# Turning attention tokens by DMA and VectorE instead of TensorE in a two-layer gated cross-attention kernel

## The chip, the cores and the metric

The kernel runs on one core of one Trainium2 chip. The metric is the device time of one execution in microseconds; lower is better. A core has a matrix engine (TensorE, PE in the profile, with its weight loads as PEld), VectorE (DVE), ScalarE (ACT), GpSimd (POOL) and SyncE (SP), which here issues every DMA. Each engine works through its own instructions in order and waits on semaphores for the others.

## The reference

Everything is float32. `x` is 8 x 512 x 512 (4096 tokens of 512 features), the context is 8 x 120 x 512. Two layers of a gated cross-attention and a gated feed-forward part follow one another; attention has 16 heads of 32.

```python
x = x + tanh(g_xattn[0]) * L0_xattn(layernorm(x), ctx, ctx, ...)
x = x + tanh(g_ffn[0])   * L0_ffn(layernorm(x), ...)       # routed experts
x = x + tanh(g_xattn[1]) * L1_xattn(layernorm(x), ctx, ctx, mask, ...)
x = x + tanh(g_ffn[1])   * L1_ffn(layernorm(x), ...)       # channel mix

# attention
q = split_heads(Q @ W_q.T); k = split_heads(K @ W_k.T); v = split_heads(V @ W_v.T)
scores = einsum('bhqd,bhkd->bhqk', q, k) / sqrt(32)
out = einsum('bhqk,bhkd->bhqd', softmax(scores), v)
return merge_heads(out) @ W_o.T
```

The second attention also has biases and a key mask. The first feed-forward part picks, in each group of 32 tokens, one token for each of 128 experts; the second mixes each token with the one before it and multiplies by three matrices.

## The kernel before

`x` stays in SBUF as 32 tiles of 128 tokens (`NT = 32`, four tiles to a batch, `TB = 4`). One class, `CrossAttention`, serves both layers: it projects keys and values first (`project_keys`, `prologue`), runs three opening slots (`slot`), 24 steady slots (`steady(k)`, k from 4 to 27) and a tail. Instructions are issued in the written order on every engine (`manual_schedule`), so the order of calls in `steady` is the order on each engine and on SP's DMA queue.

Products of 512 x 512 are done as seven quarter products with sums of quarters (`SevenProducts`). `next()` runs one product on TensorE and takes it out of PSUM; `settle()` runs GpSimd additions that belong to product 7 and were put off. In a batch's four steady slots, seven products make the queries of the next batch: two in each of the first three, one in the fourth.

A steady slot k works on several tiles at once, in this order:

- `score_products(k)` on TensorE into two PSUM tiles, then `largest` on VectorE (negated maxima, L710);
- `turn_blocks(k-1, 0)`: VectorE turns 32 x 32 blocks of one half of the probabilities of tile k-1 (L793) and SP stores them to DRAM (`plane`, L796);
- `output(k-3)`: four 128-row chunks of the product with `wo` (L878), then VectorE adds the gated result to `x` (L888);
- `exponentials` on ScalarE (L721) and `divide` (a reciprocal on VectorE, L727, a multiplication on GpSimd, L731), half 1 and then half 0, with query products between them, and `turn_blocks(k, 1)`;
- `after(..., stage)` calls the next part of the network: in the first attention `RoutedFfn.in_slot`, in the second `ChannelMix.in_slot`. For the first, stage "final" stores `x` of tile k-3 to DRAM (`put_aside`, L1046), sums its statistics and computes its scales on GpSimd (`layernorm_scales`, L61 to L64: variance plus epsilon, power, product); stage "route" does router products of earlier tiles (L1074) and transposes a tile (L1065); stage "late" scales `x` on ScalarE (`route_scale`, L1052);
- `transpose_x(k+8)`: four TensorE transpositions of the normalized tile (L588) into PSUM, and a copy by ScalarE with the factor 1/sqrt(32) (L590) into `xnT`, which feeds the query products;
- `attend(k-2)`: probabilities times values (L861), copied by ScalarE to `aT`;
- `fetch_blocks(k-1)`: four loads bring the turned probabilities back from DRAM in the transposed layout (L806, `prT`, a single buffer);
- `normalize(k+9)` on ScalarE (L564), into one of two `xn` buffers.

PSUM tiles of products, outputs, transpositions and attend share four buffers in rotation (`p_mm`, tag "mm"); the scores have two of their own. The probabilities go through DRAM for tiles 4 to 25 (`CROSSED`); for the others TensorE turns them.

Of the kernel before, what the change touches and what calls it, by code (L numbers as in the profile page):

```python
# [31 lines left out]

KB, KF = 4, 30
CROSSED = range(TB, NT - TB - 2)


class Common:
# [15 lines left out]
    cm.nc.vector.bn_aggr(cm.mv[:, t, :], st)  # L53


def layernorm_scales(cm, pool, t, n):

    nc, ts = cm.nc, slice(t, t + n)
    mean, rstd, nmr = cm.mv[:, ts, 0], cm.rstd[:, ts, 0], cm.nmr[:, ts, 0]
    ve = pool.tile([P, TB], FP, name="ve")[:, :n]  # L60
    nc.gpsimd.tensor_scalar(ve, cm.mv[:, ts, 1], EPS, None, ALU.add)  # L61
    nc.gpsimd.tensor_tensor(rstd, ve, cm.mhalf.to_broadcast([P, n]), ALU.pow)
    if n == 1:
        nc.gpsimd.tensor_scalar(nmr, mean, rstd, -1.0, ALU.mult, ALU.mult)  # L64
    else:
        nc.gpsimd.tensor_tensor(nmr, mean, rstd, ALU.mult)
        nc.gpsimd.tensor_scalar(nmr, nmr, -1.0, None, ALU.mult)


def quarter(w, c, h, n=256):  # L70
# [150 lines left out]
class CrossAttention:  # L221
# [7 lines left out]
    def __init__(  # L229
        self, cm, tc, es, ins, gate, aside, mask=None, biases=None, loads=(), then=None,  # L230
        vpool=None,
    ):
        self.cm, self.nc, self.tc, self.gate, self.then = cm, cm.nc, tc, gate, then
        self.masked, self.biased = mask is not None, biases is not None

        self.aside, self.turned = aside, not loads
        nc = cm.nc

        def pool(name, bufs, **kw):
            if kw.get("space") != bass.MemoryType.DRAM:  # L240
# [16 lines left out]
        self.ops = {}  # L257
        self.biasless, self.opening = [], True

        def right(name):  # L260
            return tc.tile_pool(name=name, bufs=1, side="right", reuse_waits="tile")

        with right("at_v") as self.vp:
            with right("at_k") as self.kp:
                self.load(ins, list(loads), mask, biases)
                if self.biased:
                    self.scale_biases()
                self.project_keys()
                if self.masked:
                    self.make_mask()  # L270
            self.work = pool("at_work", 2)
            self.prologue()
        self.late = pool("at_late", 2)

    def load(self, ins, loads, mask, biases):
# [57 lines left out]
        for _ in range(2):  # L333
            if loads:
                loads.pop(0)()
        weights(self.wq, wqT)
        for more in loads:
            more()
        weights(self.wo, woT)
# [154 lines left out]
    def prologue(self):  # L494
# [27 lines left out]
            self.transpose_x(TB + t)  # L522
            self.normalize(TB + t + 2)
        for t in self.unmeasured:
            self.stats(t)
        q.next()
        rest = self.scores(0)

# [51 lines left out]
    def transpose_x(self, t):  # L580
# [2 lines left out]
        if i == 0:  # L583
            self.xnT[b] = self.work.tile([P, NC, S + 1], FP, name="xnT")
        xn = self.xn.pop(t)
        ps = self.p_mm.tile([P, NC, P], FP, name="xnps", tag="mm")
        for c in range(NC):
            nc.tensor.transpose(ps[:, c, :], xn[:, c * P : (c + 1) * P], self.cm.ident)  # L588
        dst = self.xnT[b][:, :, i * P : (i + 1) * P]
        nc.scalar.activation(dst, ps, AF.Copy, scale=SM_SCALE)  # L590
# [197 lines left out]

    def turn_blocks(self, t, u):

        nc = self.nc
        pr = self.probs[t][:, u * 1024 : (u + 1) * 1024]
        nc.vector.transpose(pr, pr)  # L793
        if u == 1:
            self.planes[t] = self.dram.tile([KB, P, 2, 256], FP, name="plane")
        nc.sync.dma_start(  # L796
            out=self.planes[t][:, :, u, :].rearrange("k p e -> p k e"),
            in_=pr.rearrange("p (k e) -> p k e", k=KB),
        )
# [1 line left out]
    def fetch_blocks(self, t):  # L801
# [1 line left out]
        prT = self.late.tile([P, 4, 512], FP, name="prT", bufs=1)  # L803
        plane = self.planes.pop(t).rearrange("k (q f) u e -> k f q (u e)", q=4)
        for k in range(KB):
            self.nc.sync.dma_start(out=prT[k:LK:KB], in_=plane[k, :KF])  # L806
        self.probs[t] = prT

    def transpose_probs(self, t):
# [118 lines left out]
    def steady(self, k):  # L928
# [45 lines left out]
        if done is not None:  # L974
            self.after(done, "late")

    def tail(self):

        for k in range(NT - TB, NT + 2):
            self.transpose_probs_late(k - 2)  # L980
            rest = self.scores(k) if k < NT else []
            self.output(k - 3, range(NC))
            self.after(k - 3, "final")
            self.after(k, "head")
            for part in rest:
                part()
# [3 lines left out]
            self.after(k, "end")  # L990
        self.output(NT - 1, range(NC))
        self.after(NT - 1, "final")
        self.after(NT - 1, "late")
        self.after(NT + 2, "end")


class RoutedFfn:
# [42 lines left out]

    def route_stats(self, t):
        layernorm_sums(self.cm, self.route, t)
        layernorm_scales(self.cm, self.route, t, 1)

    def put_aside(self, t):
# [333 lines left out]
class ChannelMix:  # L1379
# [56 lines left out]
    def in_slot(self, s, attention, stage):  # L1436
# [7 lines left out]
        if stage == "late" and s < NT - 2 * TB:  # L1444
            attention.scales(s)
        if s == -1:
            self.start()
# [379 lines left out]
```

## Time and profile before

| what | value |
|---|---|
| median of 3 runs | 1346.75 us (1345.57 to 1349.14) |
| profiled execution: time | 1344.31 us |
| profiled execution: span from first to last instruction | 1342.5 us |
| granted TensorE clock, mean | 0.999 |
| busy share of the span | TensorE 96%, VectorE 75%, ScalarE 60%, GpSimd 52% |
| bytes moved by DMA | 160.84 MB, mean 120 GB/s |
| TensorE transpositions of tokens, L588 | 256 instructions, 38.4 us busy |
| ScalarE copies of them, L590 | 64, 39.6 us busy, 619 ns each |

Stages can be told by the score products: attention 1's steady slots run from 113.59 to 369.51 us, attention 2's end with its tail's first transpositions at 978.34 us. The routed experts lie between the two, the channel mix after them. Durations in the trace are those of single instructions or of merged runs of them ("x4"). Because matmuls are pipelined, the spacing of one group's start to the next one's start tells more of TensorE than the length shown.

### The profile page before, as it was taken

The numbers are of one execution on the slowest core, as the hardware profiler recorded it, in microseconds if no ns is written. First come the engines' busy times: TensorE is split into PE (matmuls) and PEld (weight loads), VectorE is DVE, ScalarE is ACT, GpSimd is POOL, SyncE is SP. The second block draws the span as 40 slices with busy tenths as digits, with TensorE's granted clock in tenths as the row PEclk, the third lists the DMA queues.
The fourth block names the chain that finished last, engine by engine and source line by source line (L and its number), as shares of the span: only waits on it lengthen the run. The fifth ranks groups of instructions, "written<-read, shape, count | busy, mean of one in ns | idle before, by whom it ended". The sixth has DMA issues, their size and how long they took to land. (4 is left out here: it accounts for less than half of the span.)

```text
span 1342.5 us, 32823 instructions
## 1 busy us (share of the span) xinstructions
PE 1291.0 (96%) x13184; PEld 1024.3 (76%) x13184; DVE 1002.2 (75%) x1448; ACT 807.1 (60%) x2540; POOL 704.6 (52%) x626
## 2 busy tenths in 40 slices
PE   7999999999999988999999999999999999999997
PEld 6886777777766877888888667667666888888886
DVE  5876776777685776777887687777785778787776
ACT  1368888888774445455136778888774655544442
POOL 4856655565542002555797787777664333343332
PEclk9999999999999999999999999999999999999999
DMA  9501766766603256431410077767700000000000
GB/s 313 189 1 66 224 208 204 222 211 208 198 26 111 86 171 199 128 112 63 154 47 18 33 229 214 220 212 222 223 23 1 16 17 32 32 32 32 32 32 32
DMA packets 116237, 160.84 MB, mean 120 GB/s; under 512 B 6973, under 2 KB 71997, under 8 KB 116085
## 3 DMA queue, kind: packets, MB, share of 16 engines
q1 hardware_dynamic: 116085, 158.75, 37.1%
q8 instruction: 104, 1.70, 0.5%
q14 instruction: 48, 0.39, 0.1%
HBM read 93.84 MB, written 64.88 MB: 118 GB/s over the span
## 5 line engine op out<-in xcount | busy, mean ns | idle before, releaser
L721 ACT ACTIVATE pr<-s,nmx 128x120 f32<-128x120 f32 x768 | 273.5, 498 | 43.4 <-DVE nmx L710 25.1
L878 PE MATMUL ops<-wo,aT 128*128 128x512 f32 x512 | 237.0, 604 | 3.6 <-ACT aT L869 2.3
L731 POOL TENSOR_TENSOR pr<-pr,rs 128x960 f32<-128x960 f32 x88 | 160.1, 1820 | 139.9 <-DVE rs L727 138.0
L721 ACT ACTIVATION_READ_ACCUMULATOR pr<-s,nmx 128x1 f32 x768 | 195.3, 254 | 0.0
L878 PEld LDWEIGHTS ops<-wo,aT 128*128 128x128 f32 x512 | 91.9, 189 | 99.8 <-issue 89.2
L710 DVE TENSOR_REDUCE nmx<-s 128x8 f32<-128x960 f32 x96 | 106.6, 1153 | 57.9 <-PE s L666 57.8
L1353 POOL TENSOR_TENSOR r<-r,b 128x1024 f32<-128x1024 f32 x31 | 73.5, 2377 | 145.1 <-ACT r L1352 145.1
L793 DVE STREAM_TRANSPOSE pr<-pr 128x1024 f32<-128x1024 f32 x88 | 109.1, 1240 | 37.0 <-POOL pr L731 37.0
L165 PE MATMUL qps<-xnT,wq 128*128 128x256 f32 x512 | 119.0, 380 | 0.0
L165 PEld LDWEIGHTS qps<-xnT,wq 128*128 128x128 f32 x512 | 96.3, 189 | 23.3 <-issue 10.3
L52 DVE BATCH_NORM_STATS2 bnst<-x 128x6 f32<-128x512 f32 x128 | 87.5, 684 | 0.4
L1609 POOL TENSOR_TENSOR x<-x,cv 128x512 f32<-128x512 f32 x30 | 44.0, 1466 | 79.0 <-DVE cv L1606 79.0
L759 POOL TENSOR_TENSOR pr<-pr,rs 128x960 f32<-128x960 f32 x32 | 58.1, 1823 | 40.6 <-DVE rs L758 30.8
L861 PE MATMUL aps<-prT,v 120*32 120x128 f32 x2048 | 69.2, 276 | 7.6 <-DMA prT<-plane 3.9
L888 DVE SCALAR_TENSOR_TENSOR x<-ops,gates,x 128x512 f32<-128x512 f32 x64 | 47.8, 746 | 34.5 <-PE ops L878 34.1
L666 PE MATMUL s<-kT,qT 32*128 32x120 f32 x2048 | 71.8, 276 | 0.0
L666 PEld LDWEIGHTS s<-kT,qT 32*128 32x128 f32 x2048 | 65.7, 186 | 7.0 <-issue 4.9
L861 PEld LDWEIGHTS aps<-prT,v 120*32 120x32 f32 x2048 | 52.2, 109 | 21.2 <-issue 10.7
L1352 ACT COPY r<-rps 128x1024 f32<-128x1024 f32 x31 | 31.4, 1013 | 59.1 <-PE rps L1340 59.1
L1582 ACT ACTIVATE kT<-kT 128x512 f32<-128x512 f32 x32 | 20.0, 626 | 76.2 <-DVE kT L183 41.8
L1340 PE MATMUL rps<-ident,rT 128*128 128x128 f32 x512 | 61.9, 275 | 2.0 <-DVE rT L1320 1.7
L769 ACT ACTIVATE pr<-s,nmx 128x120 f32<-128x120 f32 x128 | 44.2, 371 | 29.0 <-DVE nmx L766 29.0
(239 smaller groups left out, 3134.4 us busy)
## 6 DMA issues: line engine op xcount, KB each, us to landing
plane<-pr SPq DMA_DIRECT2D x88, 512.0 KB, 3.5
prT<-plane SPq DMA_DIRECT2D x176, 240.0 KB, 4.1
w<-in_w_dram SPq DMA_DIRECT2D x32, 512.0 KB, 5.0
x<-in_x_dram SPq DMA_DIRECT2D x8, 1024.0 KB, 16.6
aside<-x SPq DMA_DIRECT2D x32, 256.0 KB, 3.1
x<-aside SPq DMA_DIRECT2D x8, 1024.0 KB, 9.7
out_dram<-x SPq DMA_DIRECT2D x14, 512.0 KB, 2.8
wk<-in_wk_dram SPq DMA_DIRECT2D x3, 1024.0 KB, 8.8
```

Source lines behind the costliest of these rows:

```text
L52: cm.nc.vector.bn_stats(st, cm.x[:, t, :])
L165: self.nc.tensor.matmul(ps[:, m, :], rows[:, k, m * n : (m + 1) * n], columns[:, k, :], start=(k == 0), stop=(k == 1),)
L666: nc.tensor.matmul(s[j // 2][:, j % 2, hc * LK : (hc + 1) * LK], self.qT[b][r : r + 32, hc, toks], self.kT[r : r + 32, hc, keys], start=no ...
L710: nc.vector.tensor_reduce(nmx[u], sv[u], AX.X, ALU.max, negate=True)
L721: nc.scalar.activation(dst, src, AF.Exp, bias=nmx[u][:, j, hc, :], accum_out=sm[:, u, j, hc : hc + 1],)
L731: nc.gpsimd.tensor_tensor(half[u], half[u], by, ALU.mult)
L759: nc.gpsimd.tensor_tensor(pr[:, js, :, :], pr[:, js, :, :], rs[:, js, :, :].to_broadcast([P, 2, NC, LK]), ALU.mult,)
L793: nc.vector.transpose(pr, pr)
L861: nc.tensor.matmul(out, self.v[b // 2][:LK, b % 2, h * HD : (h + 1) * HD], p, start=True, stop=True,)
L878: nc.tensor.matmul(ops, self.aT[t][:, c, :], self.wo[:, c, :], start=(c == 0), stop=(c == NC - 1),)
L1340: nc.tensor.transpose(ps[:, k // 4, (k % 4) * P : (k % 4 + 1) * P], self.rT[:, 16 * tq + 8 * h + k, :], self.cm.ident,)
L1353: nc.gpsimd.tensor_tensor(r, r, b2, ALU.add)
```

## The change

For tiles 14 to 31 of each attention (`MOVED`), the transposition on TensorE and its copy on ScalarE go. Instead `normalize` also stores the normalized tile to DRAM (`rows`), a slot later four DMAs load it back with 32-token blocks moved to partitions (`move_rows`, 64 KB each in runs of 512 bytes), and a slot after that VectorE turns its 32 x 32 blocks into `xnT`. The features of `xnT` then have another order, (q j e) with e and q on partitions, so `wq` is loaded in that order in four DMAs (`load_rows`), and the remaining tiles are normalized into that order. The factor 1/sqrt(32) moves from the copy into the scales (`measure`).

Beside this: `normalize` runs for tile k+10 in slot k; the scales of stage "final" become a stage of their own, "scales", after the second `divide`; the outputs of tiles 2 and 3 are split over two slots; the store of a tile's second half of probabilities (`store_blocks(k, 1)`) is issued after `fetch_blocks(k-1)`; and each fetch takes 32 rows of 128 partitions in all, where it took 30 of 120.

```diff
+MOVED = range(3 * TB + 2, NT)
...
-def layernorm_scales(cm, pool, t, n):
+def layernorm_scales(cm, pool, t, n, shrunk=1.0):
...
-    nc.gpsimd.tensor_scalar(ve, cm.mv[:, ts, 1], EPS, None, ALU.add)
+    nc.gpsimd.tensor_scalar(ve, cm.mv[:, ts, 1], EPS, shrunk, ALU.add, ALU.mult)
...
+def load_rows(nc, w, w_in):
+
+    rows = w_in.rearrange("(q j e) f -> q e j f", q=4, j=NC)
+    for q in range(4):
+        nc.sync.dma_start(out=w[32 * q : 32 * q + 32], in_=rows[q])
...
-        weights(self.wq, wqT)
+        load_rows(nc, self.wq, wqT)
...
-                self.stats(next(self.unmeasured))
+                self.measure(next(self.unmeasured))
...
+    def measure(self, t):
+        layernorm_sums(self.cm, self.norm, t)
+        if t % TB == TB - 1:
+            layernorm_scales(self.cm, self.norm, t - TB + 1, TB, SM_SCALE**-2)
...
         xn = self.norm.tile([P, D], FP, name="xn")
+        to, x = xn, cm.x[:, t, :]
+        if t not in MOVED:
+            to = xn.rearrange("p (j q e) -> p q j e", q=4, j=NC)
+            x = x.rearrange("p (q j e) -> p q j e", q=4, j=NC)
         nc.scalar.activation(
-            xn, cm.x[:, t, :], AF.Identity, bias=cm.nmr[:, t, :], scale=cm.rstd[:, t, :]
-        )
+            to, x, AF.Identity, bias=cm.nmr[:, t, :], scale=cm.rstd[:, t, :]
+        )
+        if t in MOVED:
+            self.rows[t] = self.dram.tile([P, D], FP, name="rows")
+            nc.sync.dma_start(out=self.rows[t], in_=xn)
...
         xn = self.xn.pop(t)
-        ps = self.p_mm.tile([P, NC, P], FP, name="xnps", tag="mm")
-        for c in range(NC):
-            nc.tensor.transpose(ps[:, c, :], xn[:, c * P : (c + 1) * P], self.cm.ident)
         dst = self.xnT[b][:, :, i * P : (i + 1) * P]
-        nc.scalar.activation(dst, ps, AF.Copy, scale=SM_SCALE)
+        if t in MOVED:
+            nc.vector.transpose(
+                dst.rearrange("p j (q t) -> p q j t", q=4),
+                xn.rearrange("p (q j e) -> p q j e", q=4, j=NC),
+            )
+        else:
+            ps = self.p_mm.tile([P, NC, P], FP, name="xnps", tag="mm")
+            for c in range(NC):
+                nc.tensor.transpose(ps[:, c, :], xn[:, c * P : (c + 1) * P], self.cm.ident)
+            nc.scalar.copy(dst, ps)
+        if t not in MOVED:
+            self.open_queries(t)
...
+    def move_rows(self, t):
+
+        xn = self.norm.tile([P, D], FP, name="xn")
+        quarters = self.rows.pop(t).rearrange("(i e) (q d) -> q e i d", e=32, q=4)
+        for q in range(4):
+            self.nc.sync.dma_start(
+                out=xn[32 * q : 32 * q + 32].rearrange("p (i d) -> p i d", i=4),
+                in_=quarters[q],
+            )
+        self.xn[t] = xn
...
-            self.nc.sync.dma_start(out=prT[k:LK:KB], in_=plane[k, :KF])
+            self.nc.sync.dma_start(out=prT[k::KB], in_=plane[k])
...
         if k - 1 in CROSSED:
             self.turn_blocks(k - 1, 0)
-        done = {TB: TB - 2, TB + 1: None}.get(k, k - 3)
-        if done is not None:
-            self.output(done, range(2 if done == TB - 1 else 0, NC))
+        if k + 8 in MOVED:
+            self.transpose_x(k + 8)
+        if k > TB + 1 and k + 9 in MOVED:
+            self.move_rows(k + 9)
+        done = k - 3
+        if k > TB:
+            self.output(done, range(0 if k > TB + 2 else 2, NC))
...
         divide(0)
+        if k > TB:
+            self.after(done, "scales")
...
         self.after(k, "route")
-        if k + 8 < NT:
+        if k + 8 in MOVED:
+            self.open_queries(k + 8)
+        elif k + 8 < NT:
             self.transpose_x(k + 8)
+            if k == TB + 1:
+                self.move_rows(k + 9)
         if k == TB:
             self.attend(k - 1)
-        elif k == TB + 1:
-            self.output(TB - 1, range(2))
-        else:
+        elif k > TB + 1:
             self.attend(k - 2)
+        if k < TB + 2:
+            self.output(k - 2, range(2))
         if k - 1 in CROSSED:
             self.fetch_blocks(k - 1)
-        if k + 9 < NT:
+        if crossed:
+            self.store_blocks(k, 1)
+        if k == TB:
             self.normalize(k + 9)
-        if done is not None:
+        if k + 10 < NT:
+            self.normalize(k + 10)
+        if k > TB:
             self.after(done, "late")
...
         if stage == "final":
             self.put_aside(s)
-            self.route_stats(s)
+            layernorm_sums(self.cm, self.route, s)
+        if stage == "scales":
+            self.route_scales(s)
```

The tail calls the stage "scales" right after "final", and `ChannelMix.in_slot` computes the next layer's scales in stage "scales" where it did so in "late".

More of the change, by code (lines that the diff above doesn't have):

```diff
@@ L256, in __init__ @@
         self.wide, self.planes = [], {}
-        self.ops = {}
+        self.ops, self.rows = {}, {}
         self.biasless, self.opening = [], True
@@ L524, in prologue @@
         for t in self.unmeasured:
-            self.stats(t)
+            self.measure(t)
         q.next()
@@ L585, in transpose_x, with open_queries @@
         xn = self.xn.pop(t)
-        ps = self.p_mm.tile([P, NC, P], FP, name="xnps", tag="mm")
-        for c in range(NC):
-            nc.tensor.transpose(ps[:, c, :], xn[:, c * P : (c + 1) * P], self.cm.ident)
         dst = self.xnT[b][:, :, i * P : (i + 1) * P]
-        nc.scalar.activation(dst, ps, AF.Copy, scale=SM_SCALE)
+        if t in MOVED:
[10 more added lines that the diff above has]
+            self.open_queries(t)
+    def open_queries(self, t):
+        b, i = divmod(t, TB)
         if i == TB - 1:
@@ L789, in turn_blocks, with store_blocks @@
     def turn_blocks(self, t, u):
-        nc = self.nc
         pr = self.probs[t][:, u * 1024 : (u + 1) * 1024]
-        nc.vector.transpose(pr, pr)
+        self.nc.vector.transpose(pr, pr)
+        if u == 0:
+            self.store_blocks(t, u)
+    def store_blocks(self, t, u):
+        pr = self.probs[t][:, u * 1024 : (u + 1) * 1024]
         if u == 1:
             self.planes[t] = self.dram.tile([KB, P, 2, 256], FP, name="plane")
-        nc.sync.dma_start(
+        self.nc.sync.dma_start(
             out=self.planes[t][:, :, u, :].rearrange("k p e -> p k e"),
@@ L961, in steady @@
         self.after(k, "route")
-        if k + 8 < NT:
+        if k + 8 in MOVED:
+            self.open_queries(k + 8)
+        elif k + 8 < NT:
             self.transpose_x(k + 8)
+            if k == TB + 1:
+                self.move_rows(k + 9)
         if k == TB:
             self.attend(k - 1)
-        elif k == TB + 1:
-            self.output(TB - 1, range(2))
-        else:
+        elif k > TB + 1:
             self.attend(k - 2)
+        if k < TB + 2:
+            self.output(k - 2, range(2))
         if k - 1 in CROSSED:
             self.fetch_blocks(k - 1)
-        if k + 9 < NT:
+        if crossed:
+            self.store_blocks(k, 1)
+        if k == TB:
             self.normalize(k + 9)
-        if done is not None:
+        if k + 10 < NT:
+            self.normalize(k + 10)
+        if k > TB:
             self.after(done, "late")
@@ L983, in tail @@
             self.after(k - 3, "final")
+            self.after(k - 3, "scales")
             self.after(k, "head")
@@ L992, in tail @@
         self.after(NT - 1, "final")
+        self.after(NT - 1, "scales")
         self.after(NT - 1, "late")
@@ L1042, in route_stats, with route_scales @@
         layernorm_sums(self.cm, self.route, t)
+        self.route_scales(t)
+    def route_scales(self, t):
         layernorm_scales(self.cm, self.route, t, 1)
@@ L1443, in in_slot @@
             attention.stats(s, False)
-        if stage == "late" and s < NT - 2 * TB:
+        if stage == "scales" and s < NT - 2 * TB:
             attention.scales(s)
```

## The prediction

> **What bounds the kernel now.** I read the page's busy line first, then a table of windows by stage, then one slot of the steady loop instruction by instruction, then the lists of waits and the DMA issue rows.
>
> ```profile
> PE 1291.0 (96%) x13184; PEld 1024.3 (76%) x13184; DVE 1002.2 (75%) x1448; ACT 807.1 (60%) x2540; POOL 704.6 (52%) x626
> ```
>
> An average over stages, so the steady slots need their own table. The rows are attention 1's slots 8 to 23 and 24 to 27, then attention 2's slots 4 to 7 and 8 to 23 (window, length, busy of PE, PEld, DVE, ACT, POOL, clock, DMA share, GB/s).
>
> ```profile
> 153.50:328.55 175.05, 170.56 (x1652) 125.87 (x1649) 128.38 (x216) 145.25 (x605) 102.45 (x106) 1.00 0.65 211
> 328.55:369.51 40.96, 40.86 (x401) 29.73 (x397) 28.86 (x51) 31.47 (x143) 25.16 (x26) 1.00 0.64 200
> 751.91:789.35 37.44, 33.27 (x338) 23.63 (x338) 27.12 (x39) 29.47 (x141) 28.83 (x24) 1.00 0.45 138
> 789.35:939.60 150.25, 149.57 (x1509) 103.96 (x1506) 114.22 (x169) 123.14 (x571) 111.74 (x88) 1.00 0.71 218
> ```
>
> TensorE is 97 to 99.8% busy in the steady rows, at full clock; every other engine has slack. So TensorE's work sets the slot. Attention 1's slots 24 to 27 transpose no tokens: a control. Their first lasts 10.52 us (scores at 328.55 and 339.07) against 10.96 for the same slot with a transposition (197.59 to 208.55).
>
> The end of one slot (scores at 231.80 and 241.03), from the timeline (start, length, engine, line):
>
> ```profile
> 239.05 0.60 PE L1065 MATMUL rxps<-ident,x 128*128 128x128 f32 x4
> 239.48 0.22 POOL L61 TENSOR_SCALAR ve<-mv 128x1 f32<-128x1 f32 x1
> 239.49 0.60 PE L588 MATMUL xnps<-ident,xn 128*128 128x128 f32 x4
> 240.02 1.08 PE L861 MATMUL aps<-prT,v 120*32 120x128 f32 x32
> 240.23 0.60 ACT L590 ACTIVATE xnT<-xnps 128x512 f32<-128x512 f32 x1
> 240.46 0.27 POOL L64 TENSOR_SCALAR nmr<-mv,rstd 128x1 f32<-128x1 f32 x1
> 240.85 1.82 POOL L731 TENSOR_TENSOR pr<-pr,rs 128x960 f32<-128x960 f32 x1
> 242.37 0.80 ACT L1052 ACTIVATE x<-x,nmr,rstd 128x512 f32<-128x512 f32 x1
> 243.46 0.47 ACT L721 ACTIVATE pr<-s,nmx 128x120 f32<-128x120 f32 x1 [0.29 <-DVE nmx L710]
> ```
>
> TensorE runs without a gap. GpSimd's three small scale operations (239.48 to 240.73) lie in the hole between its two divisions, and ScalarE's scaling L1052 finds them ready.
>
> The few real TensorE waits of the two attentions, then SP's issue rows (min/median/max ns) and VectorE's block transposition:
>
> ```profile
> PE aps L861 <- DVE qT L212: 3.3, 4, 0.8
> PE aps L861 <- DMA prT<-plane: 3.9, 4, 1.7
> L806 SPq DMA_DIRECT2D prT<-plane x176: 822/838/1888, 132.9 to 972.3; - x176
> L796 SPq DMA_DIRECT2D plane<-pr x88: 359/365/564, 123.4 to 964.6; - x88
> L1046 SPq DMA_DIRECT2D aside<-x x32: 320/337/1108, 101.6 to 427.7; - x32
> L793 DVE STREAM_TRANSPOSE pr<-pr 128x1024 f32<-128x1024 f32 x88 | 109.1, 1240 | 37.0 <-POOL pr L731 37.0
> ```
>
> **The change part by part.**
>
> *TensorE transpositions.* 18 tiles in each of two attentions lose four transpositions. Their price is the control's difference, 10.96 - 10.52 = 0.44 us a tile (slot 27 against slot 23: 8.80 against 9.23). 36 x 0.435 = 15.7 us off TensorE.
>
> [...]
>
> *ScalarE.* The copy L590 (0.60 us) goes for these 36 tiles. The normalization is as many operations as before; for other tiles it writes 32-element runs. L721 writes a strided layout too, at the same 0.34 us spacing as L769's dense one, so I take nothing.
>
> *VectorE.* One block transposition of 512 elements a tile: half of L793 is 0.62 us, a dense pass such as statistics on 512 is 0.68; bounds 0.62 to 1.24 (no gain from a longer queue), taken 0.65. It sits ahead of the output's addition L888, so that addition and the first reciprocal start some 0.45 us later. VectorE's busiest steady slot is 8.59 of 11.86 us, so the work fits; the cover is TensorE's 9 to 11 us.
>
> *PSUM.* The four-buffer rotation loses one user a slot. In the third slot of each four the attend product now takes the buffer released by L212, which waits on GpSimd (3.3 us above). Without the transposition tile it takes an earlier product's buffer. Those slots last 11.86 to 12.50 us; free of the stall they would be 10.53 (slot 26 shows 10.68).
>
> *Scales behind the second division.* This adds a wait. ScalarE's L1052 needs nmr, and behind it stand the next slot's exponentials. The new cycle in attention 1, from a slot's first exponential (each piece from rows at 821.22 to 829.51, where exponentials set the pace): eight exponentials to the reciprocal 2.93, to GpSimd's start 3.21, division to 5.03, turn L793 to 6.31, reciprocal and second division to 8.29, scales 1.33 (239.40 to 240.73) to 9.62, L1052 with hand-over 0.8: 10.42 us a slot. TensorE alone would need (8.80 + 10.53 + 10.96 + 10.53)/4 = 10.2. So this cycle, not TensorE, becomes attention 1's limit. In attention 2 no L1052 follows; its scales move earlier on GpSimd, worth nothing since ScalarE already has slack.
>
> *Attention 1 summed.* Slots 4 to 27 took 369.51 - 113.59 = 255.9 us, 10.66 a slot. 24 x 10.42 = 250.1, 5.8 less; the split output removes part of slots 4 to 7's idle time (39.91 long, 37.36 busy), 2 more. I take 7.5. Bounds: nothing gained if the cycle is 10.66; 12.7 if it never binds (18 x 0.435, and the third slots' stalls: 12.50 + 11.86 + 12.50 + 11.86 - 4 x 10.96 = 4.9).
>
> *Attention 2 summed.* Slots 8 to 23: three of four last 9.73 and become 9.30. The fourth (8.05 to 8.43) cannot follow: scores to first exponential 2.7, sixteen exponentials 5.35, then the scores' PSUM is free: 8.05. A cycle goes from 150.25/4 = 37.56 to 27.9 + 8.05 + 0.1 for a later VectorE = 36.05; times four, 6.0. Slots 4 to 7 idle 4.2 us: 1.38 for exponentials in the slot without output, which now gets half of one, 1.66 for a fetch that stood behind a store now queued after it. I take 3.0. Together 9.0; bounds 3 to 12.5.
>
> *SP's queue.* Each steady slot gains a store of rows, which waits for the normalization, and four loads, which wait for that store to land and for VectorE to release the tile; behind them stand put_aside and the four probability fetches, and TensorE's attend waits for these. The loop on SP is four fetches, two probability stores, a rows store, its landing, four loads, in attention 1 a put_aside. For the eight 32-partition issues the near rows are 0.34 (128 partitions) and 0.84 (30 partitions at a step of four): 2.7 to 6.7 us. With 0.72 for the stores, 0.34, and a landing of 3.1 (aside's median): 6.9 to 10.9. I take 0.36 apiece, since the loads have unit step and the fetch loses its odd 30: 7.0, below the 9.0 us slot; the cover is TensorE. The data, four times 0.26 MB of fetch, 1.05 MB stored, 0.52 MB new, is 2.6 MB a slot; at the 350 GB/s of 238 to 240 us it is 7.5 us, so that fits, with little to spare.
>
> [...]
>
> *The rest.* wq's load in four pieces of 256 KB, the same bytes, is needed some 30 us after it is issued; the zero rows add 64 KB to a fetch. I charge 0.5 us, bounds 0 to 2.
>
> Sum: 7.5 + 9.0 - 0.5 = 16 us. The profiled execution took 1344.31 us (span 1342.5, 1.8 around it), so it would take 1328.3; the median of the runs is 1346.75, 2.4 above it. I forecast 1346.75 - 16 = 1331.
>
> **The rivals.**
> - *TensorE stays the bound everywhere*, the scales' cycle overlaps better than I think: 12.7 + 12 = 24.7 us, 1322. For it: GpSimd is 59% busy there. Against: every piece of the cycle is in order on its engine.
> - *The scales' cycle eats attention 1's gain* (10.66 or more) and attention 2 gets only its 6: 1341. For it: ScalarE then idles in front of L1052.
> - *SP becomes the bound, slower.* If an issue of 32 partitions costs 0.84, the loop is 10.9 us in attention 2 against 9.4 now: 18 x 1.5 = 27 lost; attention 1's 11.2 against 10.66 loses 18 x 0.55 = 10: 1384. It decides from 8x + 4.16 = 9.4, x = 0.65 us. For it: prT's row; against: all rows with 128 partitions and unit step.
> - *The turn by VectorE does not shorten anything* because its tile arrives late: loads issued some 5.5 us into a slot must land by 4.7 us into the next, 8 us later; landings in the trace are at most 5.4. A slot without gain is 1346.
>
> **How the numbers follow.** Forecast (1326 to 1337) 0.46; TensorE bound throughout 0.18; cycle eats it 0.13; no gain 0.06; SP bound or another new stall 0.17. A change of 0.3%, 4 us, is about what a measurement of this kernel can tell from none. So faster 0.76, same 0.07, slower 0.17. The range takes 1318 (both upper bounds, 25, and 4 for stalls not listed) to 1347.
>
> **What would show it.** Right: L588 down from 256 to 112 instructions, spacing of scores in attention 2 at 9.30 three times of four; in attention 1 ScalarE waiting in front of L1052 for nmr, and a mean spacing near 10.4. Transposition near 0.65 us; the 32-partition issues near 0.36. Wrong: TensorE waiting for prT, VectorE waiting for xn from a DMA, SP's issues back to back, or spacing above 9.73 in attention 2.

## The result, and the profile after

The change made the kernel slower: 1393.66 us (median of 4 runs, 1391.38 to 1395.27) beside 1347.45 us for the kernel before in the same comparison, ratio 1.0343 [1.0329, 1.0357]. The forecast was 1331 us and faster. The profiled execution took 1391.38 us, with a span of 1389.4 us and a mean granted clock of 0.978 (0.999 before).

The busy line of the page, after:

```profile
PE 1301.3 (94%) x13040; PEld 1023.9 (74%) x13040; DVE 1018.5 (73%) x1484; ACT 788.1 (57%) x2504; POOL 702.3 (51%) x626
```

TensorE has 144 instructions fewer, as it should, and yet more busy time. The table of windows says where; attention 1's slots 8 to 23, then attention 2's, after (columns as in the prediction's table):

```profile
156.20:346.98 190.78, 173.28 (x1589) 125.01 (x1585) 135.78 (x229) 135.68 (x594) 101.54 (x105) 0.96 0.75 244
807.86:985.95 178.09, 156.30 (x1444) 104.86 (x1442) 124.05 (x186) 116.66 (x556) 111.52 (x89) 0.91 0.74 234
```

Against 175.05 and 150.25 us these stretches lost 15.7 and 27.8 us. In the second, TensorE idles 21.8 us where it idled 0.7. Its busy time should have fallen by 16 x 0.435 = 7.0 us and rose by 6.7, so an estimate puts 13.7 us of it down to the lower clock (0.91), by the price of 0.435. In the first, 13.0 us are added idle time and, by the same estimate, 9.7 the clock (0.96). Slots 4 to 7 lost 2.65 and 2.77 us, slots 24 to 27 1.1 and 0.4; the part between the two attentions gained 3.8. Together this is the 46.9 us of the span.

What TensorE waits for, from the list of waits of PE and then of SP's queue (us in total, times, longest), after:

```profile
PE aps L909 <- DMA prT<-plane: 24.4, 14, 3.1
```

```profile
SPq L633 <- DMA rows<-xn: 119.6, 33, 4.7
SPq L854 <- DMA plane<-pr: 28.6, 11, 6.0
```

TensorE waits for the fetched probabilities (3.9 us before). They come late because SP, in front of the loads L633, waits 33 times in 36 for the rows that it has just stored. One round of SP's queue in attention 1, from the timeline, after (start, length, line):

```profile
231.21 1.74 SPq L633 DMA_DIRECT2D xn<-rows  x4
233.05 0.38 SPq L1113 DMA_DIRECT2D aside<-x  x1
233.54 2.53 SPq L854 DMA_DIRECT2D prT<-plane  x4
236.17 1.36 SPq L844 DMA_DIRECT2D plane<-pr  x1
237.63 0.45 SPq L586 DMA_DIRECT2D rows<-xn  x1
238.17 1.20 SPq L844 DMA_DIRECT2D plane<-pr  x1
242.21 1.75 SPq L633 DMA_DIRECT2D xn<-rows  x4
```

It is busy back to back from 231.21 to 239.37 us. Then comes the hole, from 239.37 to 242.21: the store of 237.63 must land before the loads may go. The time from the start of a DMA's issue until its data have arrived is called its landing, 4.5 us here. The round closes on itself (loads, fetch, store, rows, landing, loads) and lasts 11.0 us here, with no TensorE in it. ScalarE had the tile ready long before the store's turn came; its normalization ended at 234.04, 3.6 us ahead of 237.63:

```profile
233.23 0.81 ACT L581 ACTIVATE xn<-x,nmr,rstd 128x512 f32<-128x512 f32 x1
```

Issue rows of the four (min/median/max ns), after, and the landing row of the rows' store (last number: median us):

```profile
L633 SPq DMA_DIRECT2D xn<-rows x144: 303/426/1666, 132.9 to 977.6; - x144
L854 SPq DMA_DIRECT2D prT<-plane x176: 577/603/1627, 135.6 to 1019.5; - x176
L844 SPq DMA_DIRECT2D plane<-pr x88: 359/539/1722, 123.4 to 1011.6; - x88
L586 SPq DMA_DIRECT2D rows<-xn x36: 320/448/942, 126.0 to 971.4; - x36
```

```profile
rows<-xn SPq DMA_DIRECT2D x36, 256.0 KB, 5.3
```

The loop by these rows: 4 x 0.43 + 4 x 0.60 + 2 x 0.54 + 0.45 + 5.3 = 10.95 us in attention 2, 11.3 with the put_aside in attention 1. The mean slots were 178.09/16 = 11.13 and 190.78/16 = 11.92.

### The profile page after: what moved, and what is told of

Read it like the earlier page. It is cut to its first block, busy times and chain, and to the rows that moved or that the text cites. A ratio compares the mean times of both kernels' runs of the same rounds, so it can differ in the third digit from the quotient of the medians.

```text
span 1389.4 us, 32889 instructions
## 1 busy us (share of the span) xinstructions
PE 1301.3 (94%) x13040; PEld 1023.9 (74%) x13040; DVE 1018.5 (73%) x1484; ACT 788.1 (57%) x2504; POOL 702.3 (51%) x626
## 5 line engine op out<-in xcount | busy, mean ns | idle before, releaser
L764 ACT ACTIVATE pr<-s,nmx 128x120 f32<-128x120 f32 x768 | 273.4, 497 | 45.9 <-DVE nmx L753 33.4
L926 PE MATMUL ops<-wo,aT 128*128 128x512 f32 x512 | 248.5, 627 | 3.6 <-ACT rxT L1134 1.5
L926 PEld LDWEIGHTS ops<-wo,aT 128*128 128x128 f32 x512 | 96.1, 199 | 105.8 <-issue 95.2
L909 PE MATMUL aps<-prT,v 120*32 120x128 f32 x2048 | 74.6, 290 | 38.0 <-DMA prT<-plane 24.4
L909 PEld LDWEIGHTS aps<-prT,v 120*32 120x32 f32 x2048 | 56.5, 115 | 55.6 <-issue 27.4
L709 PEld LDWEIGHTS s<-kT,qT 32*128 32x128 f32 x2048 | 74.3, 205 | 9.7 <-issue 7.1
L709 PE MATMUL s<-kT,qT 32*128 32x120 f32 x2048 | 80.6, 296 | 0.3 <-ACT pr L764 0.3
L917 ACT COPY aT<-aps 128x512 f32<-128x512 f32 x64 | 38.6, 603 | 46.4 <-PE aps L909 46.3
```

The costliest lines, as they stand in the source:

```text
L709: nc.tensor.matmul(s[j // 2][:, j % 2, hc * LK : (hc + 1) * LK], self.qT[b][r : r + 32, hc, toks], self.kT[r : r + 32, hc, keys], start=no ...
L764: nc.scalar.activation(dst, src, AF.Exp, bias=nmx[u][:, j, hc, :], accum_out=sm[:, u, j, hc : hc + 1],)
L909: nc.tensor.matmul(out, self.v[b // 2][:LK, b % 2, h * HD : (h + 1) * HD], p, start=True, stop=True,)
L926: nc.tensor.matmul(ops, self.aT[t][:, c, :], self.wo[:, c, :], start=(c == 0), stop=(c == NC - 1),)
```

## The experiments

All edits are made on the changed kernel unless another is named. Where an expectation names a theory by a letter: A is the rows' landing on SP's queue, C the scales' cycle through GpSimd, B the amount of data on the DMA engines, D the store of the second half behind the fetch, F the split outputs. Slot sums are us from one slot's scores to a later slot's, each from the profiled execution; ratios are to the kernel before, measured in the same comparison. A profiled execution is one of several and lies up to 6.4 us above its kernel's median (e4, e7) or 4.7 below it (e6). Stages that an edit doesn't touch differ by up to 3.1 us between two profiles (attention 2's slots 8 to 23 in e7 and e8), so a smaller difference of one stage settles nothing by itself.

| kernel | median us | ratio | att. 1, 8-23 | att. 2, 4-7 | att. 2, 8-23 |
|---|---|---|---|---|---|
| before | 1347.45 | 1 | 175.05 | 37.44 | 150.25 |
| changed | 1393.66 | 1.0343 [1.0329, 1.0357] | 190.80 | 40.21 | 178.09 |
| e1_fixed_rows | 1359.88 | 1.0082 [1.0065, 1.0098] | 172.46 | 40.89 | 165.30 |
| e2_early_norm | 1351.32 | 1.0026 [1.0008, 1.0044] | 169.47 | 40.03 | 157.23 |
| e3_no_moved | 1360.40 | 1.0081 [1.0060, 1.0103] | 174.57 | 40.56 | 157.60 |
| e4_scales_back | 1393.09 | 1.0339 [1.0312, 1.0366] | 191.29 | 39.83 | 181.11 |
| e5_no_moved_store | 1353.48 | 1.0043 [1.0030, 1.0055] | 174.72 | 40.33 | 150.47 |
| e6_early_store | 1353.71 | 1.0027 [1.0013, 1.0041] | 168.29 | 45.03 | 152.55 |
| e7_early_store_out | 1349.72 | 1.0005 [0.9986, 1.0024] | 168.23 | 44.20 | 156.04 |
| e8_early_store_out_scales | 1347.31 | 0.9985 [0.9963, 1.0007] | 165.57 | 42.44 | 159.13 |
| e9_first_only | 1334.38 | 0.9909 [0.9892, 0.9926] | 163.96 | 37.51 | 150.66 |
| e10_rows_act | 1352.61 | 1.0047 [1.0030, 1.0064] | 170.89 | 39.37 | 159.50 |
| e11_all_back_rows_act | 1341.71 | 0.9953 [0.9933, 0.9972] | 165.49 | 42.38 | 150.26 |
| e12_first_fetch | 1343.78 | 0.9957 [0.9943, 0.9971] | 167.40 | 42.79 | 148.30 |

**e1_fixed_rows: the loads without the landing in front of them.** The same stores and loads, but every load reads the rows of tile 12, written once; the moved tiles thus hold tile 12's tokens, and no load depends on the store of the slot before.

```diff
+        self.once = pool("at_once", 1, space=bass.MemoryType.DRAM)
...
+        if t == 12:
+            self.fixed = self.once.tile([P, D], FP, name="fixed")
+            nc.sync.dma_start(out=self.fixed, in_=xn)
...
-        quarters = self.rows.pop(t).rearrange(...)
+        self.rows.pop(t)
+        quarters = self.fixed.rearrange(...)
```

> The change, but the four loads of each tile read one DRAM tile that was written once in the opening slots (tile 12's normalized rows), so that SP does not wait for the landing of the store of the slot before. Stores, bytes, run lengths and number of issues stay; the moved tiles' contents are wrong. Theory A (SP's in-order queue: the wait for the landing, 3.2 us in the median, stands at the head of put_aside and the fetches and makes a loop of 11 us): attention 2's mean slot falls from 11.1 to 9.0-9.4 us, attention 1's from 11.9 to 10.2-10.7, time 1325-1345 us. Rival B (22 MB more on the DMA engines are too much): waits for prT stay, time 1380-1395. Rival C (the scales behind the second division hold ScalarE): attention 1 stays near 11.9, attention 2 is not touched, time 1380-1395.

Measured: 1359.88 us, 33.8 less than the changed kernel. The edit takes only the wait away (one more store of 256 KB comes in), so the wait for the landing holds most of the loss. It is not all: the time stays above the 1325 to 1345 us expected and above the kernel before, and SP now waits 70.0 us in front of the fetch for the plane store.

**e2_early_norm: the rows stored earlier in the slot.** The tile is normalized and its rows stored ahead of stage "route".

```diff
         self.q7.settle()
+        if k > TB and k + 10 < NT:
+            self.normalize(k + 10)
         self.after(k, "route")
...
-        if k + 10 < NT:
+        if k == TB:
             self.normalize(k + 10)
```

> The change, but in slots 5 and later the normalization of tile k+10 and the store of its rows are issued before the stage route, ahead of the fetch of the probabilities and of the second half's store, instead of behind both. Nothing is left out. Theory A: the rows have landed long before the next slot's loads ask, SP waits under 0.5 us there, attention 2's mean slot 9.0-9.4, attention 1's 10.2-10.7, time 1325-1345 us; ScalarE gets 0.8 us of work ahead of the copies, at most 0.4 us in the fourth slot of four. Rival B: no difference, 1380-1395. Rival C: attention 1 stays near 11.9, time 1380-1395.

Measured: 1351.32 us, above the 1325 to 1345 expected, but 42 below the changed kernel by an edit of place alone. The store now lands after 2.9 us (median) instead of 5.3, behind other work, and SP no longer waits for it: the list of SP's waits has no row of L633 for the rows, where the changed kernel's has 119.6 us. The bytes moved are the same, so rival B does not hold these 42 us.

**e3_no_moved: all of the change but the moved tiles.**

```diff
-MOVED = range(3 * TB + 2, NT)
+MOVED = range(NT, NT)
...
-            if k == TB + 1:
-                self.move_rows(k + 9)
```

> The change without its main part: no tile is turned by DMA (all 32 by TensorE, as before); normalization two tiles ahead, the late scales, the split outputs, the new order on SP, the 32-row fetches and the permuted layout stay. Theory A and rival B: what is left costs little, attention 2's mean slot 9.3-9.5, time 1338-1350 us. Rival C: attention 1's mean slot 11 or more, time 1352-1365.

Measured: 1360.40 us, 0.8% slower than before without a moved tile, where 1338 to 1350 was expected. From the list of waits of SP's queue, of this kernel:

```profile
SPq L854 <- DMA plane<-pr: 154.9, 64, 6.3
```

In front of the fetches SP stands until a plane store has landed, 154.9 us in all. Attention 1's slots 8 to 23 lose nothing by it (174.57 us), attention 2's lose 7.4. So the parts around the moved tiles have a cost of their own.

**e4_scales_back: the scales again at "final", with all the rest.**

```diff
         if stage == "final":
             self.put_aside(s)
-            layernorm_sums(self.cm, self.route, s)
-        if stage == "scales":
-            self.route_scales(s)
+            self.route_stats(s)
```

> The change with the first network's scales back ahead of the second division (stage final), all else as in the change. Theory A: attention 1 is held by SP, not by the scales, at most 4 us less: 1388-1394 us. Rival C: attention 1 falls from 11.9 to 10.9 a slot, 16 us less: 1374-1380. Attention 2 is not touched by this edit under either.

Measured: 1393.09 us, no change. While SP sets the slot the scales' wait is hidden.

**e5_no_moved_store: e3 with the second half's store back ahead of the fetch.**

```diff
     def turn_blocks(self, t, u):
...
-        if u == 0:
-            self.store_blocks(t, u)
+        self.store_blocks(t, u)
...
-        if crossed:
-            self.store_blocks(k, 1)
```

> No tile turned by DMA, and the store of a tile's second half of probabilities again issued as soon as it is turned, ahead of the fetch, as before the change; the rest of the change stays. Theory D (the new place of that store lets the fetch wait for a store that was issued late and stands behind 1.5 MB in the queues: 155 us of SP waits for plane in e3): SP's waits for plane fall under 20 us, attention 2's slots 8 to 23 from 157.6 to 150-151 us, time 1349-1353 us. Rival E (the split outputs and the order of slots 4 to 7 are all of it): slots 8 to 23 stay at 157, time 1358-1361.

Measured: 1353.48 us, and attention 2's slots 8 to 23 fall from 157.60 to 150.47, to what they were before. SP's waits for the plane are nearly gone, of this kernel:

```profile
SPq L853 <- DMA plane<-pr: 1.9, 2, 1.4
```

Issued behind the fetch (e3), the second half lands too late for the next slot's fetch: SP waited 154.9 us there and waits 1.9 here. That is D. What stays of 0.4% lies outside these slots: slots 4 to 7 take 2.4 us more than before in attention 1 and 2.9 in attention 2 (there 2.5 of it are busy time, at a clock of 0.92 instead of 1.00).

**e6_early_store: e2 with the same store edit as e5.**

```diff
# on e2
-        if u == 0:
-            self.store_blocks(t, u)
+        self.store_blocks(t, u)
...
-        if crossed:
-            self.store_blocks(k, 1)
```

> e2 (rows normalized and stored ahead of the fetch) with that store back ahead of the fetch too. Theory D: attention 2's slots 8 to 23 from 157.2 to 144-149 us, time 1336-1345 us. Rival E: 157 stays, time 1349-1353. Rival B (bytes): fetches arrive late in any order, 155 or more, time over 1348.

Measured: 1353.71 us: a miss, and not below e2's 1351.32. Attention 2's slots 8 to 23 gained 4.7 us (152.55, where 144 to 149 was expected), but slot 6 there grew from 12.6 to 16.3 us, and slots 4 to 7 took 5.0 back.

**e7_early_store_out: e6 with the outputs of tiles 2 and 3 where they were before.**

```diff
# on e6
-        done = k - 3
-        if k > TB:
-            self.output(done, range(0 if k > TB + 2 else 2, NC))
+        done = {TB: TB - 2, TB + 1: None}.get(k, k - 3)
+        if done is not None:
+            self.output(done, range(2 if done == TB - 1 else 0, NC))
...
-        if k < TB + 2:
-            self.output(k - 2, range(2))
+        elif k == TB + 1:
+            self.output(TB - 1, range(2))
```

> e6 with the outputs of tiles 2 and 3 in the slots where they were before the change. Theory F (the split outputs leave TensorE idle in slots 4 to 7: 42.9 us in e2 against 39.9 before in attention 1, 40.0 against 37.4 in attention 2, and a lower clock there): slots 4 to 7 return to 38-40 and 35-38 us, time 3-6 us below e6. Rival: those slots are held by the first loads and fetches, time within 1.5 us of e6.

Measured: 1349.72 us, 4.0 below e6 as F had it, though the intervals of the two overlap; but slots 4 to 7, where F put the gain, hardly move (42.76 to 42.88 in attention 1, 45.03 to 44.20 in attention 2). With moved tiles the split outputs do not hold them long, and F falls there.

**e8_early_store_out_scales: e7 with the scales back at "final".**

```diff
# on e7
-            layernorm_sums(self.cm, self.route, s)
-        if stage == "scales":
-            self.route_scales(s)
+            self.route_stats(s)
```

> e7 with the first network's scales back ahead of the second division. Theory C (scales, scaling of x and exponentials make a cycle of 10.4 us in attention 1): ScalarE's waits for nmr vanish (37 us in e2), attention 1's slots 8 to 23 from about 168 to 163-165 us, time 4-6 us below e7. Rival (TensorE's stall behind product 4 comes back, 4 x 1.2 us): within 1.5 us of e7 or slower.

Measured: 1347.31 us, 2.4 less than e7, where intervals overlap; but attention 1 shows it in its slots, 168.23 to 165.57 in 8 to 23 and 42.88 to 40.56 in 4 to 7. ScalarE's wait for nmr falls from 40.2 to 3.8 us. So C is real. Together these slots give 5 us; the stretch of 8 to 23 alone, 2.7 us, is within the spread of profiles, but the pattern is plain: the second slot of four takes 11.7 to 12.1 us in e7, from slot 9 on, and 10.96 in e8 from slot 13 on. The time of the whole kernel fell by less than the 4 to 6 us expected.

**e9_first_only: e8 with moved tiles in attention 1 alone.**

```diff
# on e8
+        self.moved = MOVED if loads else range(NT, NT)
...
-        if t in MOVED:
+        if t in self.moved:
...
-        if k > TB and k + 10 < NT:
+        if self.moved and k > TB and k + 10 < NT:
             self.normalize(k + 10)
```

In attention 2 it normalizes tile k+9 in its old place.

> Tiles turned by DMA in the first attention alone, rows normalized and stored ahead of the fetch (as e2), the second half's store, the outputs and the scales in their places of before; the second attention transposes on TensorE, normalizes one tile ahead, and keeps the permuted layout and the 32-row fetch. If theory A, C and D hold together: attention 1 as in e8 (slots 4 to 27 about 249 us against 257.8 before), attention 2 as before (slots 8 to 23 150 us, slots 4 to 7 37-38), time 1336-1341 us against 1347 before. Rival B (bytes on the DMA engines hold even the first attention): attention 1 at 255 or more, time 1345 or more.

Measured: 1334.38 us (1333.88 to 1335.21), faster than both kernels by more than the interval, and a little better than expected. The window of attention 1's slots 8 to 23, of this kernel:

```profile
156.69:320.65 163.96, 163.47 (x1588) 118.95 (x1584) 134.72 (x229) 135.82 (x588) 101.62 (x105) 1.00 0.86 283
```

TensorE is 99.7% busy at full clock in 163.96 us. The rival "TensorE stays the bound everywhere" put this stretch at 175.05 less 16 x 0.435 less 4.9 for the third slots: 163.2.

**e10_rows_act: the changed kernel, with the rows' store issued on ScalarE's queue.**

```diff
-            nc.sync.dma_start(out=self.rows[t], in_=xn)
+            nc.scalar.dma_start(out=self.rows[t], in_=xn)
```

> The change with one edit: the store of the normalized rows is issued on ScalarE's DMA queue instead of SP's, so that it does not stand behind the fetches and the second half's store in SP's order; bytes and all other orders stay. Theory A: the landing falls from 5.3 us to 2.0-3.5, SP's waits for rows from 120 us to under 30, time 1350-1365 us (the store of the second half behind the fetch still costs what e3 showed). Rival B: landings stay over 5 us since the engines are full, time 1385-1395.

Measured: 1352.61 us, 41 less. The landing row and SP's waits, of this kernel:

```profile
rows<-xn ACTq DMA_DIRECT2D x36, 256.0 KB, 3.6
```

```profile
SPq L844 <- DMA rows<-xn: 28.0, 12, 5.2
SPq L633 <- DMA rows<-xn: 4.9, 5, 1.7
```

The store has the same bytes, and lands after 3.6 us instead of 5.3, a little above what was expected. It is also issued earlier, and by more than that. In the changed kernel SP comes to it 4.1 us after the normalization has ended (median of 36); here ScalarE issues it as soon as it is done:

```profile
233.89 0.81 ACT L581 ACTIVATE xn<-x,nmr,rstd 128x512 f32<-128x512 f32 x1
234.74 0.33 ACTq L586 DMA_DIRECT2D rows<-xn  x1
```

So the run tests the store's place in the order of issue and its queue together, and not the queue alone; e2, on SP's queue, got as much from the place. In front of the loads SP waits 4.9 us instead of 119.6; the trace puts 28.0 us in front of a plane store down to the same landing, which leaves 32.9 in all. One word undoes nearly all of the loss.

**e11_all_back_rows_act: e8 with the rows' store on ScalarE's queue.**

```diff
# on e8
-            nc.sync.dma_start(out=self.rows[t], in_=xn)
+            nc.scalar.dma_start(out=self.rows[t], in_=xn)
```

> e8 (both attentions turned by DMA, rows early, second half's store, outputs and scales in their places of before) with the rows' store on ScalarE's DMA queue. If attention 2's slots 8 to 23 (159 us in e8, 150 before) are held by the rows' store standing ahead of the fetch on SP: 144-150 us, time 1332-1340. If they are held by the amount of data between one attend and the next (rival B, for attention 2 alone): 155-160 us, time 1344-1352.

Measured: 1341.71 us, between the two expectations. Attention 2's slots 8 to 23 fall from 159.13 to 150.26: the rows' store on SP did hold them. But 150.26 is only what they took before, though TensorE is 142.74 us busy there (149.57 before). Its 7 us came off and turned into idle time. And slots 4 to 7 stay at 42.38.

**e12_first_fetch: e11 with the first moved tile's loads behind the first fetch.**

```diff
# on e11
-            if k == TB + 1:
-                self.move_rows(k + 9)
...
             self.fetch_blocks(k - 1)
+            if k == TB + 1:
+                self.move_rows(k + 9)
```

> The kernel before this one (all parts undone but the moved tiles, rows stored by ScalarE's queue) with one edit: in the fifth slot of the steady loop the four loads of the first moved tile are issued behind the fetch of the probabilities instead of ahead of it. In that kernel attention 2's slots 4 to 7 took 42.38 us against 37.44 before, all of it in slot 6 (16.4 against 10.4), where TensorE waited 4.51 us for the first fetch, issued at 768.41 behind loads that took 2.17 us. If the loads ahead of the first fetch are the cause: the fetch is issued some 2.2 us earlier and lands without the loads' data in front of it, slot 6 falls to 11 to 13 us, attention 2's slots 4 to 7 to 37.5 to 39.5, and the time from 1341.7 to 1337 to 1339. If the cause is the store in front of them (the second half's store of tile 5, which VectorE turns late), slot 6 stays above 15 us and the time at 1340 to 1343. Attention 2's slots 8 to 23 stay at 150 in either case, since nothing in them is changed.

Measured: 1343.78 us (1340.27 to 1346.60), the same as e11. (Slot 6 took 11.5 us in the kernel before; the expectation's 10.4 is e9's.) Slot 6 of attention 2 falls from 16.4 to 14.0, between the two expectations, and slot 7 rises from 9.2 to 12.1. The fetch starts at 766.48 us instead of 768.41, and still TensorE waits. From the timelines of TensorE and SP, of this kernel:

```profile
773.31 1.93 PE L908 MATMUL aps<-prT,v 120*32 120x128 f32 x32 [3.71 <-DMA prT<-plane]
```

```profile
753.48 12.83 SPq L843 DMA_DIRECT2D plane<-pr  x3
```

The delay is moved, not removed. The stores ahead of the fetch end at 766.31, and the third of them waits for VectorE's turn of tile 5, which waits for GpSimd. In e9 the same three end 19.4 us behind slot 4's scores, here 21.8. GpSimd's timeline shows where these 2.4 us come from; here, and then in e9:

```profile
757.76 4.96 POOL L597 TENSOR_TENSOR x<-x,gbo 128x512 f32<-128x512 f32 x4
764.68 1.25 DVE L835 STREAM_TRANSPOSE pr<-pr 128x1024 f32<-128x1024 f32 x1 [4.75 <-POOL pr L774]
```

```profile
755.29 2.52 POOL L598 TENSOR_TENSOR x<-x,gbo 128x512 f32<-128x512 f32 x2
```

In the second attention each call of `normalize` also puts up to two additions of the output's bias on GpSimd (`add_bias`), ahead of the division that the turn waits for. Slot 4 calls it for tiles k+9 and k+10, so four additions stand there; e9's attention 2 calls it for one tile, and two do. The later turn thus comes from the normalization two tiles ahead and not from the moved tiles: e3 and e5, without any, have the same four additions. No run moved them, so what they cost in time is not shown.

## Why the prediction was wrong

**The step that failed** is the sum of SP's loop, 8x + 4.16 = 7.0 us, set below the slot of 9.0 so that SP cost nothing; the loop took 11 us and became the slot. Within it the term most short is the landing. It was taken as 3.1 us, the median of all put_asides; those of the steady slots stand some 1.0 us behind half a plane and 2.8 us behind the last of four fetches, and landed after 2.0 to 4.4, 3.4 in the median. The rows' store stands closer, mostly 0.6 us behind half a plane and 1.3 us behind a fetch of 1.05 MB, and landed after 5.3. The other terms were short too:

| term of the loop | predicted us | measured us | share of the miss |
|---|---|---|---|
| landing of the rows | 3.1 | 5.3 | 2.2 |
| eight issues of 32 partitions | 2.9 | 4.1 | 1.2 |
| two plane stores and a rows store | 1.06 | 1.53 | 0.5 |
| loop | 7.0 | 10.95 | 3.9 |

The landing is counted from the start of the issue. So the rows' own issue, and the next slot's first-half store that SP issues while it waits, lie inside it, and this sum counts them twice, as the prediction's did. By the timeline, attention 2's fifteen rounds from 800.57 to 971.41 us took 11.4 us each: 5.5 landing, 2.2 loads, 2.6 fetch, 0.8 from the fetch to the next rows' store, 0.3 between.

The rival "SP becomes the bound, slower" was the right one, for another reason than its own. It was to decide from x = 0.65 us; the mean of the eight issues is 0.51. With a landing of 3.1 the measured round would be some 11.4 - 2.4 = 9.0 us, an estimate, as long as the slot; no run shortened the landing inside the loop. What the runs show is the wait: e1 and e2 take the landing out of SP's loop, e10 nearly all of it, and 34, 42 and 41 of the 46 us came back. The prediction's own bounds for the loop, 6.9 to 10.9, reached above the slot already, with the landing held at 3.1; it took the lower end and called the rest cover.

**The new queue order had the wrong sign.** The prediction priced the second half's store behind the fetch as a gain of 1.66 us in attention 2's slots 4 to 7. e3 against e5, one edit apart, shows its cost: 7.1 us in attention 2's slots 8 to 23. It asked what the fetch gains and not who waits for the store: the next slot's fetch.

**TensorE's 15.7 us** were right as work. TensorE's busy time fell by 6.8 us in e11's sixteen slots, beside 7.0 by the price of 0.435. They became time in attention 1 alone (e9). There the steady slots, up to the tail's first transpositions, took 8.5 us less than before (247.4 beside 255.9; 7.5 forecast), but with the scales in their old place; with the late scales e6 and e7 have 2.8 and 2.7 us less.

**VectorE's block transposition** was taken as 0.65 us and took 0.67:

```profile
L608 DVE STREAM_TRANSPOSE xnT<-xn x36: 662/669/714, 142.7 to 980.1; 128x512 f32<-128x512 f32 x36
```

**The scales' cycle** of 10.42 us a slot was right as a limit and near in the mean, hidden in the changed kernel (e4) and seen in e7: 168.23/16 = 10.51. It is not an even 10.42, though: the second slot of every four takes 11.7 to 12.1 us where e9 has 10.96, and the others soon last what they last in e9. Putting the scales back gives 10.35 (e8) and 10.25 (e9, the same code in attention 1). So a part of the change worked against the gain.

**PSUM's third slots** lost their stall as forecast: attention 1's slots 10, 14, 18 and 22 took 12.50 and 11.86 us by turns and take 10.7 and 10.5 in e7 and e9 (10.53 forecast).

**Attention 2's 9.0 us** failed. Its cycle was to be three slots of 9.30 and one of 8.05. In e12's slots 8 to 23, eight of sixteen last 9.3 and the fourth ones 8.0 to 9.0, so the prices hold; but four last 9.5 to 10.4, and 148.30 us, in the fastest of twelve executions, is 2.0 less than before instead of 6.0. The 3.0 us of slots 4 to 7 never came: 40.3 to 40.6 us without any moved tile (e3, e5), above 37.44. e9's attention 2, with the outputs whole and one tile normalized ahead, is back at 37.51, so these two parts lengthen the slots together; which does how much was not tested. (In the prediction's table this row is 89% busy, 33.27 of 37.44, and not 97.)

**The fetch of 32 rows** fell from 0.84 to 0.60 us an issue, not to the 0.36 of the stores. That the odd 30 rows made the difference was the author's estimate, which no run shows: none changes the number of rows by itself. In place of the 0.36 us taken for all eight issues of 32 partitions, the median was 0.60 for the fetches and 0.43 for the loads at unit step; the plane stores took 0.54 in this kernel.

**What stays open:** why attention 2 keeps so little in slots 8 to 23, where TensorE idles 7.5 us in e11 and 4.6 in e12. In e11 and e12 its DMA share is 0.85 to 0.86, and so it is in e9's attention 1, which has its gain in full; a bound by the amount of data alone is therefore not shown. The single buffer prT was not tried with two.

## What to carry to other kernels

Before a load is put behind a store on the same queue, write the queue's loop with the landing in it, and take that landing from a store with as much data as close in front of it, not from a median over all moments (3.1 us was taken, 5.3 measured); a cover of 2 us in 9 needs both ends of every term. A store whose landing is waited for should be issued as soon as its data are ready, on another engine's queue (e10, 41 us less) or earlier on the same one (e2, 42 us less), so that its landing lies under other work. When several edits come together, take them one by one: here the moved tiles of one layer (e9: -0.9%) were a gain, and the rows' store behind the fetch, the new order of the plane stores, the later scales and the other layer's moves took it back.

## What the runs showed of the hardware

In attention 2 of the changed kernel TensorE's granted clock fell after short gaps, here from 1.00 to 0.72 after one of 2.2 us (columns as above; the eighth number is the clock):

```profile
881.40:883.62 2.22, 0.00 (x0) 0.03 (x1) 1.52 (x3) 0.00 (x0) 1.92 (x2) 1.00 1.02 353
883.62:884.85 1.23, 1.23 (x37) 1.03 (x40) 0.00 (x0) 0.09 (x1) 1.06 (x3) 1.00 1.01 368
884.85:891.00 6.15, 6.15 (x45) 3.57 (x38) 3.96 (x4) 4.27 (x20) 3.62 (x5) 0.72 0.43 130
```

After 2.22 us without an instruction the clock holds for another 1.2 us and is then 0.72 over the next 6; the same 32 score products take 1.87 us where they took 1.05 one slot earlier:

```profile
873.26 1.05 PE L709 MATMUL s<-kT,qT 32*128 32x120 f32 x32
884.85 1.87 PE L709 MATMUL s<-kT,qT 32*128 32x120 f32 x32
```

In attention 2's slots 8 to 23 the clock fell five times, each time within 4 us of the start of a gap of 2.2 to 3.1 us. A gap of 2.38 us that ended at 872 us had no such effect, nor one of 2.85 us at 982, so the length of one gap does not settle it. In slots 8 to 23 of both attentions an estimate puts 23.4 us down to the lower clock, beside 34.1 of added idle time (together 57.5, less the 14.0 of work taken off, for a loss of 43.6): each microsecond of added waiting came with 0.7 more. That the gaps cause the fall is read from the order of the rows, not tested by itself; the same stretch at 99.7% busy (e9, attention 1) has a clock of 1.00.

The landing of the rows' store differed with its place. The same 256 KB landed after 5.3 us (median) close behind the fetch and half a plane on SP's queue, 2.9 ahead of the fetch on that queue (e2; 3.7 in e9), and 3.6 on ScalarE's queue (e10). The queue's own part in it was not separated.
